# Norm factors by root and reciprocal, and small moves on GpSimd and VectorE, in a graph attention block that searches 64 MB of adjacency

## The chip, the cores and the metric

The kernel runs on one core of a Trainium2 chip. The metric is the device time of one execution in microseconds, taken as the median of three runs. Beside it stands one execution that the hardware profiler recorded; its span reaches from the first to the last instruction of the program.

## The reference, cut to what matters

```python
# x: 4096 x 512, adj: 4096 x 4096, W: 512 x (4 heads * 512), a: 4 x 1024 x 1
ht  = (h @ W).reshape(N, 4, 512).transpose(1, 0, 2)
src = einsum('hnd,hd->hn', ht, a[:, :512, 0]); dst = einsum('hnd,hd->hn', ht, a[:, 512:, 0])
e   = leaky_relu(src[:, :, None] + dst[:, None, :], 0.01) + adj[None]
h_prime = einsum('hij,hjd->hid', softmax(e, -1), ht).mean(0)
out = layernorm(x + h_prime)          # per row, eps 1e-5
```

The entries of adj reach 1e9, so in nearly every row the largest one outweighs everything else in the softmax, which is then one at a single column. The kernel computes that case: for every row i it finds the column c(i) of the largest entry of adj, fetches row c(i) of x, multiplies it by the mean of the four heads' weights, adds x and normalises. It also bounds how large the attention scores can be (from the norms of x, of W per head, and of a) and counts the rows whose lead over the second largest entry is too small for this. Only if there is one does it branch to `general`, which computes whole softmaxes. With these inputs the branch is not taken.

## The kernel before, in words

The 4096 rows are 32 blocks of 128 rows. Block 0 holds the rows 0 to 127; of the others, partition p holds 31 consecutive rows, one for each block. The scheduling is by hand: every engine runs its instructions in the order in which the program issues them, and the main loop is `for t in range(NB)` (line 523), a software pipeline of 32 steps. Step t does, in this order:

- SyncE (SP queue) issues the load of block t + 5 of adj (`load_adj`; 2 MB, in two pieces from block 28, in four for block 31) and, at some steps, four blocks of x (`load_x`) into `hold`, a tile that keeps all 32 blocks of x and later of the output. Six buffers hold adj.
- VectorE (DVE) reduces block t of adj to the maxima of segments of 16, 32 or 64 entries (`segment_maxima`, line 203: two instructions a block, four for block 31), finds the largest segment (`find_segment`, lines 210 and 212), and, in step t, looks for the column within the fetched segment of block t - 2 (`find_column`, line 263). In the steps of `END` the column comes after the segment, otherwise between the two reductions.
- GpSimd (POOL) works out the address of the leading segment and fetches it again from HBM with an indirect DMA (`fetch_segment`, lines 219 to 230), and, when the column is known, gathers the rows of x (`gather_rows`, lines 239 or 248). Two dependent indirect DMAs thus stand between the search of a block and its matmuls.
- TensorE (PE) turns the gathered rows of block t - 3 (`turn`, line 277; ScalarE copies the result to SBUF, line 279), adds x through the identity (`residual`, line 289) and multiplies by the mean weights (`products`, line 296: four matmuls of 128 x 512 in float32).
- ScalarE (ACT) takes the sums of squares for the bound (`row_norm`) and, in `parked_stats`, moves the result of block t - 4 into `hold` and takes its mean and variance.
- Every fourth step from step 8, `rstd` makes the factors 1/sqrt(var + eps) of four blocks with four POOL operations (lines 366 to 370, the power at line 367), and `finish` (line 375, ACT) normalises block t - 9.

Blocks 1 to 17 (`TABLED`) treat the first 128 rows of x apart, which are the columns found most often: the product of these 128 rows with the weights is kept in `z`, a one-hot matmul (`spread`, `from_table`) picks from it, and the gather skips these columns. To skip them, `gather_rows` adds 8192 to such a column (lines 245 and 247), so that it lies out of bounds and is not fetched.

The last blocks have their own order, written out after the loop (lines 586 to 652). Blocks 24 to 27 are put by (`put_by`) and get x by an addition on POOL or DVE (`add_x`, line 350), blocks 28 to 31 get their statistics on DVE (`moments`, `normalise`). The column of block 31 is searched in its whole row (line 271). The norms of heads for the bound (`head_norms`) are done in three parts in steps 24, 26 and 28, each behind the segment search. All stores stand behind the last loads on the SP queue; the last one is that of block 31.

Of the kernel before, what the change touches and what calls it, by code (L numbers as in the profile page):

```python
# [72 lines left out]
def leading_rows(ctx, tc, x, adj, W, a, out, ident, n_bad, any_bad):  # L73
# [44 lines left out]
    def pieces(ib):  # L118
        return PIECES if ib == NB - 1 else 2 if ib >= LATE else 1
# [55 lines left out]
    nc.gpsimd.iota(nth, pattern=[[0, 1]], base=0, channel_multiplier=-1)  # L175
# [20 lines left out]
    def segment_maxima(ib, lo, hi):  # L196

        e = spans[span_of(ib)][0]
        if lo == 0:
            seg_of[ib] = small.tile([P, N // e], F32, name=f"seg{e}", bufs=2)  # L200
        n = max(pieces(ib), 2)
        for k in range(lo * n // PIECES, hi * n // PIECES):
            nc.vector.tensor_reduce(  # L203
                seg_of[ib][:, ts(k, N // e // n)],
                adj_t[ib][:, ts(k, N // n)].rearrange("p (s e) -> p s e", e=e), axis=AX.X, op=OP.max,
            )
# [9 lines left out]
    def fetch_segment(ib):  # L216
        at = at_of.pop(ib)
        row = small.tile([P, 1], U32, name="row")
        nc.gpsimd.tensor_tensor(row, at[:, 0:1], first[:, ib : ib + 1], op=OP.add)  # L219
        k = span_of(ib)  # L220
        e = spans[k][0]
        lead = lead_pool.tile([P, e], F32, name=f"lead{e}", bufs=LEADS[k])
        nc.gpsimd.indirect_dma_start(  # L223
            out=lead, out_offset=None, in_=adj_segs[e],
            in_offset=bass.IndirectOffsetOnAxis(ap=row[:, :1], axis=0),
        )
        lead_of[ib] = lead
        if ib < NB - 1:
            start = at_of[ib] = small.tile([P, 1], U32, name="start")
            nc.gpsimd.tensor_tensor(start, at[:, 0:1], width[:, k : k + 1], op=OP.mult)  # L230
# [5 lines left out]
    def gather_rows(ib, col):  # L236
        if ib not in TABLED:
# [6 lines left out]
        away = small.tile([P, 1], U32, name="away")  # L244
        nc.gpsimd.tensor_scalar(away, col, float(P), float(SKIP), op0=OP.is_lt, op1=OP.mult)
        there = small.tile([P, 1], U32, name="there")
        nc.gpsimd.tensor_tensor(there, col, away, op=OP.add)  # L247
        nc.gpsimd.indirect_dma_start(  # L248
            out=y_t[ib], out_offset=None, in_=x,
            in_offset=bass.IndirectOffsetOnAxis(ap=there[:, :1], axis=0),  # L250
# [3 lines left out]
        nc.gpsimd.tensor_scalar(low, col, float(P), None, op0=OP.min)  # L254
# [109 lines left out]

    def rstd(i):
        nc.gpsimd.tensor_scalar(sd[:, i], sd[:, i], 1.0 / D, EPS, op0=OP.mult, op1=OP.add)
        nc.gpsimd.tensor_tensor(sd[:, i], sd[:, i], power[:, : i.stop - i.start], op=OP.pow)  # L367
        nc.gpsimd.tensor_mul(nm[:, i], nm[:, i], sd[:, i])
        if i.stop <= BEHIND:
            nc.gpsimd.tensor_scalar(sd[:, i], sd[:, i], -float(D), None, op0=OP.mult)  # L370

    def finish(ib):
        i = slice(ib, ib + 1)
        o = hold[:, ib, :] if ib < BEHIND else o_ps.pop(ib)
        nc.scalar.activation(hold[:, ib, :], o, AF.Identity, bias=nm[:, i], scale=sd[:, i])  # L375
# [144 lines left out]
    COLUMN, PROJECT, STATS, FINISH = 2, 3, 4, 8  # L520
    END = (*range(1, 3), *range(5, 20))

    for t in range(NB):
# [7 lines left out]
        middle = 1 if t == NB - 1 else 2  # L531
# [3 lines left out]
        segment_maxima(t, middle, PIECES)  # L535
# [8 lines left out]
        if t >= FINISH and t % Q == 0:  # L544
            rstd(slice(t - FINISH, t - FINISH + Q))
# [8 lines left out]
        if t in (24, 26, 28):  # L554
            head_norms((t - 24) // 2)
# [27 lines left out]
        if t > FINISH:  # L583
            finish(t - FINISH - 1)
# [36 lines left out]
    rstd(slice(BEHIND, BEHIND + 3))  # L621
# [34 lines left out]
def general(ctx, tc, x, adj, W, a, out, ident, n_bad):  # L656
# [21 lines left out]
    with ExitStack() as pre:  # L678
# [7 lines left out]
        for g in range(NCH):  # L686
            nc.gpsimd.dma_start(x_sb[:, ts(g, Q), :], x_blocks[:, ts(g, Q), :])
# [145 lines left out]
```

## Time and profile before

| | |
|---|---|
| median of three runs | 234.69 us (234.55 to 234.91) |
| the profiled execution's own time | 234.5 us |
| its span | 233.0 us |
| mean granted TensorE clock | 0.975 |
| busy: PE, DVE, ACT, POOL | 194.3, 191.1, 139.8, 112.9 us |
| moved by DMA | 96.45 MB, mean 414 GB/s |
| read from HBM, written to it | 88.54 MB, 8.39 MB |

A row of the profile names a line, an engine, an operation and its tiles as out<-in, then times in microseconds from the start of the span. Idle time before an instruction stands in brackets with what ended it. Rows of a group give the count, the busy time and the mean of one instruction in nanoseconds.

### The profile page before, as it was taken

The page shows a single profiled execution, that of the slowest core. Times are in us where ns is not written, and L with a number is a line of the kernel's source. Part 1 is how long each engine was busy: PE and PEld are TensorE (multiplying, and loading weights), DVE is VectorE, ACT ScalarE, POOL GpSimd, SP SyncE. Part 2 cuts the span into 40 slices and gives each one's busy share as a digit, 9 for nine tenths or more (in the row PEclk, how much of TensorE's full clock was granted, in tenths as well). Part 3 has the DMA queues.
Part 4 walks back from the last instruction along what each step waited for, and adds up shares of the span by engine and source line. Part 5 has one row for each costly group of instructions (what it writes and reads, how often), then busy time and mean ns, then how long its engine had stood idle before and what let it go on. Part 6 is the DMA issues. An engine that isn't in the chain of part 4 may idle for free.

```text
span 233.0 us, 2399 instructions
## 1 busy us (share of the span) xinstructions
PE 194.3 (83%) x570; PEld 92.6 (40%) x576; DVE 191.1 (82%) x301; ACT 139.8 (60%) x340; POOL 112.9 (48%) x260
## 2 busy tenths in 40 slices
PE   0069988789099996999899999999999977899990
PEld 0024443334044443445344444544443433345460
DVE  0448299899969997999799958977999999988782
ACT  3002213588077775699798767767756763289761
POOL 4020415615554875467657755653465447557210
PEclk9999999999769998899999999999999999999998
DMA  6999999999999999999999999999999999999985
GB/s 229 433 422 437 420 437 421 438 427 414 436 431 420 422 433 434 427 421 434 423 426 424 432 429 427 420 430 430 429 432 413 427 422 425 410 425 418 424 357 203
DMA packets 12834, 96.45 MB, mean 414 GB/s; under 512 B 2087, under 2 KB 2535, under 8 KB 7056
## 3 DMA queue, kind: packets, MB, share of 16 engines
q1 hardware_dynamic: 9216, 88.08, 89.5%
q0 software_dynamic: 3584, 8.16, 8.9%
q8 instruction: 5, 0.08, 0.1%
q14 instruction: 13, 0.11, 0.1%
q10 hardware_dynamic: 16, 0.02, 0.0%
HBM read 88.54 MB, written 8.39 MB: 416 GB/s over the span
## 4 chain that ended last, share of the span: by engine, by line
DMA 64%; DVE 19%; PE 6%; ACT 4%; issue 3%; POOL 1%; SPq 0%; DVEq 0%; POOLq 0%
DMA adj_t<-in_adj_dram 56%; DVE seg L203 16%; DMA hold<-in_L_gnn_W_dram 5%; PE o L296 4%; DMA y<-in_x_dram,col 3%; ACT sq L340 2%; PE o L384 2%; DVE at L212 1%; ACT hold L375 1%; DVE top L210 1%; PE tp L277 1%; DVE within L263 1%; POOL sd L367 0%; POOL lead L223 0%; ACT yt L279 0%
## 5 line engine op out<-in xcount | busy, mean ns | idle before, releaser
L203 DVE TENSOR_REDUCE seg<-adj_t 128x128 f32<-128x2048 f32 (+3 forms) x66 | 144.1, 2210 | 29.8 <-DMA adj_t<-in_adj_dram 29.7
L296 PE MATMUL o<-w_sum,yt 128*128 128x512 f32 x248 | 114.4, 602 | 2.0 <-ACT yt L279 1.8
L296 PEld LDWEIGHTS o<-w_sum,yt 128*128 128x128 f32 x248 | 46.3, 193 | 54.9 <-issue 42.6
L279 ACT COPY yt<-tp 128x512 f32<-128x512 f32 x33 | 19.1, 579 | 34.3 <-PE tp L277 34.3
L223 POOL DMA_INDIRECT lead<-in_adj_dram,row x32 | 32.6, 1020 | 13.1 <-POOL row L219 13.1
L277 PE MATMUL tp<-ident,y 128*128 128x128 f32 x128 | 22.5, 300 | 15.9 <-DMA y<-in_x_dram,there 12.0
L219 POOL TENSOR_TENSOR row<-at,first 128x1 uint32<-128x1 uint32 x32 | 6.1, 191 | 54.0 <-DVE at L212 45.4
L277 PEld LDWEIGHTS tp<-ident,y 128*128 128x128 f32 x128 | 18.7, 208 | 30.5 <-issue 27.0
L435 PE MATMUL o<-hold,ident 128*128 128x512 f32 x32 | 17.0, 699 | 13.7 <-DMA hold<-in_L_gnn_W_dram 13.7
L289 PE MATMUL o<-hold,ident 128*128 128x512 f32 x52 | 27.5, 614 | 0.0
L248 POOL DMA_INDIRECT y<-in_x_dram,there x17 | 18.9, 1111 | 10.9 <-POOL there L247 5.6
L340 ACT ACTIVATE sq<-hold 128x512 f32<-128x512 f32 x32 | 19.9, 624 | 0.0
L375 ACT ACTIVATE hold<-hold,nm,sd 128x512 f32<-128x512 f32 x24 | 19.1, 802 | 0.0
L239 POOL DMA_INDIRECT y<-in_x_dram,col x15 | 14.9, 995 | 7.6 <-POOL col L265 7.0
L363 ACT ACTIVATE sq<-hold,nm 128x512 f32<-128x512 f32 x24 | 17.4, 724 | 0.8
L435 PEld LDWEIGHTS o<-hold,ident 128*128 128x128 f32 x32 | 7.1, 226 | 22.8 <-issue 22.3
L436 ACT ACTIVATE w_sum<-o 128x512 f32<-128x512 f32 x4 | 2.4, 597 | 22.9 <-PE o L435 22.9
L326 ACT ACTIVATE off<-px,minus 128x128 f32<-128x128 f32 x17 | 6.3, 368 | 15.3 <-PE px L324 15.3
L361 ACT ACTIVATE hold<-o 128x512 f32<-128x512 f32 x24 | 14.3, 597 | 0.8
L336 PE MATMUL o<-z,pick 128*128 128x512 bf16 x46 | 13.9, 407 | 0.2
L210 DVE MAX8 top<-seg 128x8 f32<-128x256 f32 (+2 forms) x32 | 11.6, 361 | 1.1
L212 DVE FIND_INDEX8 at<-top,seg 128x8 uint32<-128x256 f32 (+2 forms) x32 | 11.3, 352 | 0.0
(113 smaller groups left out, 178.7 us busy)
## 6 DMA issues: line engine op xcount, KB each, us to landing
adj_t<-in_adj_dram SPq DMA_DIRECT2D x28, 2048.0 KB, 33.0
hold<-in_x_dram SPq DMA_DIRECT2D x6, 1024.0 KB, 32.4
adj_t<-in_adj_dram SPq DMA_DIRECT2D x6, 1024.0 KB, 28.1
hold<-in_L_gnn_W_dram SPq DMA_DIRECT2D x2, 2048.0 KB, 16.6
out_dram<-hold SPq DMA_DIRECT2D x7, 512.0 KB, 5.4
out_dram<-hold SPq DMA_DIRECT2D x3, 1024.0 KB, 15.1
adj_t<-in_adj_dram SPq DMA_DIRECT2D x4, 512.0 KB, 19.8
hold<-in_x_dram SPq DMA_DIRECT2D x2, 512.0 KB, 14.4
```

The source lines that it names most:

```text
L203: nc.vector.tensor_reduce(seg_of[ib][:, ts(k, N // e // n)], adj_t[ib][:, ts(k, N // n)].rearrange("p (s e) -> p s e", e=e), axis=AX.X, op ...
L223: nc.gpsimd.indirect_dma_start(out=lead, out_offset=None, in_=adj_segs[e], in_offset=bass.IndirectOffsetOnAxis(ap=row[:, :1], axis=0),)
L239: nc.gpsimd.indirect_dma_start(out=y, out_offset=None, in_=x, in_offset=bass.IndirectOffsetOnAxis(ap=col[:, :1], axis=0),)
L248: nc.gpsimd.indirect_dma_start(out=y_t[ib], out_offset=None, in_=x, in_offset=bass.IndirectOffsetOnAxis(ap=there[:, :1], axis=0), bounds_c ...
L277: nc.tensor.transpose(tp[:, kb, :], y[:, ds(kb, P, KB)], ident)
L279: nc.scalar.copy(yt, tp)
L289: nc.tensor.matmul(o_ps[ib], ident, hold[:, ib, :], start=start, stop=False)
L296: nc.tensor.matmul(o_ps[ib], yt_of[ib][:, kb, :], w_sum[:, kb, :], start=(start and kb == 0), stop=(kb == KB - 1),)
L340: nc.scalar.activation(sq, hold[:, ib, :], AF.Square, accum_out=xx[:, ib : ib + 1])
L363: nc.scalar.activation(sq, hold[:, ib, :], AF.Square, bias=nm[:, i], scale=-float(D), accum_out=sd[:, i])
L375: nc.scalar.activation(hold[:, ib, :], o, AF.Identity, bias=nm[:, i], scale=sd[:, i])
L435: nc.tensor.matmul(o, ident, hold[:, w_at + kb * H + h, :], start=(h == 0), stop=(h == H - 1))
```

## The change

1. **Factors.** `rstd` no longer takes a power on POOL. A new `root` issues a square root on ACT behind the statistics; three steps later `rstd` issues a reciprocal on DVE and two operations on POOL. The groups are blocks 0 to 3, 4 to 7, 8 to 11, 12 to 15, 16 to 19, and then 20 and 21, 22 and 23; their reciprocals stand in steps 10, 14, 18, 22, 26, 28 and 30. `finish` comes two steps later, with two blocks each in steps 28 and 29. Blocks 24 to 26 keep the power (`late_factors`).
2. **Skip with the segment.** For blocks 1 to 17 the 8192 is added to the segment's start in `fetch_segment` if the whole segment lies in the first 128 columns. The column then carries it, and the two operations in front of the gather go away. The one-hot pick is shifted by one to suit.
3. **Norms of heads** in steps 21, 22 and 23.
4. **Whole searches.** In steps 12 to 19 one reduction takes the whole block of adj.
5. In `general`, x is loaded in 16 pieces, not 8.

The diff, cut to its core:

```diff
-    nc.gpsimd.iota(nth, pattern=[[0, 1]], base=0, channel_multiplier=-1)
+    nc.gpsimd.iota(nth, pattern=[[0, 1]], base=-1, channel_multiplier=-1)
...
-        n = max(pieces(ib), 2)
+        n = max(pieces(ib), 1 if ib in WHOLE else 2)
...
-            nc.gpsimd.tensor_tensor(start, at[:, 0:1], width[:, k : k + 1], op=OP.mult)
+            if ib in TABLED:
+                away = small.tile([P, 1], F32, name="away")
+                nc.gpsimd.tensor_scalar(away, at[:, 0:1], float(P // e), float(SKIP), op0=OP.is_lt, op1=OP.mult)
+                nc.gpsimd.tensor_scalar(start, at[:, 0:1], float(e), away, op0=OP.mult, op1=OP.add)
+            else:
+                nc.gpsimd.tensor_tensor(start, at[:, 0:1], width[:, k : k + 1], op=OP.mult)
...
-        away = small.tile([P, 1], U32, name="away")
-        nc.gpsimd.tensor_scalar(away, col, float(P), float(SKIP), op0=OP.is_lt, op1=OP.mult)
-        there = small.tile([P, 1], U32, name="there")
-        nc.gpsimd.tensor_tensor(there, col, away, op=OP.add)
...
-        nc.gpsimd.tensor_scalar(low, col, float(P), None, op0=OP.min)
+        nc.gpsimd.tensor_scalar(low, col, float(SKIP - 1), float(SKIP - 1), op0=OP.max, op1=OP.subtract)
...
+    def root(i):
+        nc.scalar.activation(sd[:, i], sd[:, i], AF.Sqrt, bias=eps, scale=1.0 / D)
+
     def rstd(i):
+        nc.vector.reciprocal(sd[:, i], sd[:, i])
+        nc.gpsimd.tensor_mul(nm[:, i], nm[:, i], sd[:, i])
+        nc.gpsimd.tensor_scalar(sd[:, i], sd[:, i], -float(D), None, op0=OP.mult)
+
+    def late_factors(i):
         nc.gpsimd.tensor_scalar(sd[:, i], sd[:, i], 1.0 / D, EPS, op0=OP.mult, op1=OP.add)
         nc.gpsimd.tensor_tensor(sd[:, i], sd[:, i], power[:, : i.stop - i.start], op=OP.pow)
         nc.gpsimd.tensor_mul(nm[:, i], nm[:, i], sd[:, i])
-        if i.stop <= BEHIND:
-            nc.gpsimd.tensor_scalar(sd[:, i], sd[:, i], -float(D), None, op0=OP.mult)
...
-    COLUMN, PROJECT, STATS, FINISH = 2, 3, 4, 8
+    COLUMN, PROJECT, STATS, BEHIND_ROOT = 2, 3, 4, 3
+    FACTORS = (*((lo, lo + Q) for lo in range(0, BEHIND - Q, Q)), (BEHIND - 4, BEHIND - 2), (BEHIND - 2, BEHIND))
+    FINISHED = {t: (t - 11,) for t in range(11, 28)}
+    FINISHED |= {28: (17, 18), 29: (19, 20), 30: (21,), 31: (22,)}
+    WHOLE = range(12, 20)
...
-        middle = 1 if t == NB - 1 else 2
+        middle = PIECES if t in END else 1 if t == NB - 1 else 2
...
-        segment_maxima(t, middle, PIECES)
+        if t not in END:
+            segment_maxima(t, middle, PIECES)
...
-        if t >= FINISH and t % Q == 0:
-            rstd(slice(t - FINISH, t - FINISH + Q))
+        for lo, hi in FACTORS:
+            if t == hi - 1 + STATS + BEHIND_ROOT:
+                rstd(slice(lo, hi))
...
-        if t in (24, 26, 28):
-            head_norms((t - 24) // 2)
+        if 21 <= t < 24:
+            head_norms(t - 21)
...
-        if t > FINISH:
-            finish(t - FINISH - 1)
+        for lo, hi in FACTORS:
+            if t == hi - 1 + STATS:
+                root(slice(lo, hi))
+        for done in FINISHED.get(t, ()):
+            finish(done)
...
-    rstd(slice(BEHIND, BEHIND + 3))
+    late_factors(slice(BEHIND, BEHIND + 3))
...
-        for g in range(NCH):
-            nc.gpsimd.dma_start(x_sb[:, ts(g, Q), :], x_blocks[:, ts(g, Q), :])
+        for g in range(0, NB, 2):
+            nc.gpsimd.dma_start(x_sb[:, ds(g, 2), :], x_blocks[:, ds(g, 2), :])
```

More of the change, by code (lines that the diff above doesn't have):

```diff
@@ L243, in gather_rows @@
             return
-        away = small.tile([P, 1], U32, name="away")
-        nc.gpsimd.tensor_scalar(away, col, float(P), float(SKIP), op0=OP.is_lt, op1=OP.mult)
-        there = small.tile([P, 1], U32, name="there")
-        nc.gpsimd.tensor_tensor(there, col, away, op=OP.add)
         nc.gpsimd.indirect_dma_start(
             out=y_t[ib], out_offset=None, in_=x,
-            in_offset=bass.IndirectOffsetOnAxis(ap=there[:, :1], axis=0),
+            in_offset=bass.IndirectOffsetOnAxis(ap=col[:, :1], axis=0),
             bounds_check=N - 1, oob_is_err=False,
```

## The prediction

> **What bounds the kernel now.** I read the page first: its span and the row of DMA shares over 40 slices.
>
> ```profile
> span 233.0 us, 2399 instructions
> DMA  6999999999999999999999999999999999999985
> ```
>
> The sixteen DMA engines are at 90% or more in every slice except the first and the last two. Then the windows (columns after the window: its length, busy time and count of PE, weight loads, DVE, ACT and POOL, the granted clock, the DMA share, GB/s):
>
> ```profile
> 140.00:170.00 30.00, 29.71 (x91) 14.29 (x89) 26.01 (x42) 20.61 (x51) 14.33 (x29) 1.00 1.01 427
> 205.00:210.00 5.00, 4.74 (x14) 2.21 (x14) 4.62 (x10) 4.78 (x14) 2.46 (x4) 1.00 1.03 420
> 220.00:225.00 5.00, 5.00 (x19) 2.92 (x18) 4.46 (x10) 3.04 (x8) 1.28 (x3) 1.00 0.95 397
> 225.00:229.00 4.00, 2.27 (x11) 1.66 (x9) 2.92 (x12) 2.25 (x6) 0.00 (x0) 1.00 0.83 326
> 229.00:233.00 4.00, 0.00 (x0) 0.00 (x0) 0.15 (x1) 0.30 (x1) 0.00 (x0) 0.81 0.35 135
> ```
>
> The DMA share is full until about 220 us and falls only after that, to 0.83 and 0.35. The change moves no bytes. So time that an engine saves before the last rows of adj have landed is not time saved: DVE, idle for 4 of 30 us in the first window, would only wait longer for its rows. What counts is the order of events at the end, and there PE is the full engine (5.00 of 5.00). The chain that ended last says how PE's last work was released (start, us, what):
>
> ```profile
> 193.55 0.20 POOL start L230
> ...
> 193.84 0.20 POOL sd L366
> ...
> 194.11 1.06 POOL sd L367
> ...
> 195.24 0.20 POOL nm L368
> ...
> 195.52 0.23 POOL sd L370
> 195.76 0.17 POOL col L265
> ...
> 196.59 6.92 DMA y<-in_x_dram,col
> ...
> 203.64 0.72 PE tp L277 x4
> ...
> 223.73 3.55 PE o L384 x16
> ```
>
> This is step 28. POOL computes the factors of blocks 20 to 23 (L366 to L370) between the segment fetch of block 28 and the column of block 27. The gather of block 27 leaves behind them at 196.59, lands at 203.51, and PE turns block 27 at 203.64. From there PE runs almost without a gap to 227.28, the end of the last row. A gain at the end must pass here.
>
> **The change part by part.** *The factors of step 28.* Before, POOL is held from 193.84 to 195.76, 1.92 us, of which the power (L367) is 1.06. After, this step has two blocks and two POOL operations (L368 and L370, 0.20 and 0.23, with a gap of about 0.08 before each), behind a reciprocal on DVE. POOL, free at 193.75, is done with them at 194.26. The column then waits for DVE, whose search ends thus:
>
> ```profile
> 194.21 0.18 DVE L263 FIND_INDEX8 within<-top,lead 128x8 uint32<-128x32 f32 x1
> ...
> 200.44 0.96 POOL L239 DMA_INDIRECT y<-in_x_dram,col  x1 [0.54 <-POOL col L265]
> ```
>
> Search done at 194.39, column 0.07 later and 0.19 long, 0.54 from column to gather as in the second row: the gather of block 27 leaves at 195.2 rather than 196.59, and at 194.9 with the 0.3 us that DVE gains below. With its 6.92 us it lands at about 201.9. PE can take it no sooner than its residuals end:
>
> ```profile
> 200.67 1.88 PE L289 MATMUL o<-hold,ident 128*128 128x512 f32 x4
> ```
>
> They end at 202.55, so PE gains 1.09 us at block 27, and 1.3 if the gather of block 26, on which these residuals hang, lands earlier by DVE's 0.2 to 0.3.
>
> *DVE in the last steps.* A search (L212) and the adj reduction behind it, without and with the norms of heads between them:
>
> ```profile
> 180.62 0.28 DVE L212 FIND_INDEX8 at<-top,seg 128x8 uint32<-128x128 f32 x1
> ...
> 181.16 2.28 DVE L203 TENSOR_REDUCE seg<-adj_t 128x64 f32<-128x2048 f32 x1
> ...
> 186.30 0.28 DVE L212 FIND_INDEX8 at<-top,seg 128x8 uint32<-128x128 f32 x1
> 186.50 2.27 DVE L203 TENSOR_REDUCE seg<-adj_t 128x32 f32<-128x2048 f32 x1
> ...
> 191.56 0.22 DVE L212 FIND_INDEX8 at<-top,seg 128x8 uint32<-128x64 f32 x1
> ...
> 191.95 2.28 DVE L203 TENSOR_REDUCE seg<-adj_t 128x32 f32<-128x2048 f32 x1
> ```
>
> Step 27 has none: 0.20 from search to reduction, 0.14 for the shorter search of the last blocks (0.22 instead of 0.28). Step 26 has 0.54 and step 28 has 0.39: the parts moved away give back 0.34 and 0.25. The reciprocals come in at steps 26, 28 and 30:
>
> ```profile
> L404 DVE RECIPROCAL sd<-sd 128x1 f32<-128x1 f32 x5 | 0.8, 156 | 0.8 <-ACT sd L401 0.7
> ```
>
> I take 0.13 for each, since operations here start before the one ahead has quite ended; 0.16 at most for one column, and four columns should not be dearer by more than a few hundredths. So DVE is ahead by 0.2 after step 26, 0.3 after step 28, 0.2 after step 30. Each reciprocal waits for a root issued three steps earlier, which ACT finished about two steps before (a step is 5.4 us, from 186.50 to 191.95 above), so nothing is queued behind it. The three L203 rows bear no idle mark, so DVE does not wait for adj in these steps and the 0.3 us is real; it ends where the last quarter of block 31 lands.
>
> *The gate of block 29.* The new factors of step 30 (blocks 22, 23) stand before the column of block 29 on POOL:
>
> ```profile
> 204.24 0.20 POOL L230 TENSOR_TENSOR start<-at,width 128x1 uint32<-128x1 uint32 x1
> 204.67 0.19 POOL L265 TENSOR_TENSOR col<-start,within 128x1 uint32<-128x1 uint32 x1 [0.23 <-DVE within L263]
> 205.40 0.96 POOL L239 DMA_INDIRECT y<-in_x_dram,col  x1 [0.54 <-POOL col L265]
> 207.87 1.28 POOL L350 TENSOR_TENSOR adj_t<-adj_t,hold 128x512 f32<-128x512 f32 x1 [1.51 <-ACT sq L340]
> ...
> 214.31 0.96 POOL L239 DMA_INDIRECT y<-in_x_dram,col  x1 [0.61 <-PE tp L277]
> ```
>
> The start operation moves 0.3 earlier with DVE, to 203.94 to 204.14; two factor operations with their gaps (0.59) end at 204.73; column 0.19, then 0.54: gather at 205.46, against 205.40 before. Its landing time:
>
> ```profile
> DMA to landing us min/median/max: 7.0/7.0/7.0
> ```
>
> It lands at 212.5, and PE can turn block 29 then rather than at
>
> ```profile
> 213.07 0.63 PE L277 MATMUL tp<-ident,y 128*128 128x128 f32 x4
> ...
> 222.24 0.63 PE L277 MATMUL tp<-ident,y 128*128 128x128 f32 x4
> ```
>
> 213.07. Of the 1.1 to 1.3 us that PE gained, about 0.5 passes this gate. ACT, full in 205 to 210 (4.78 of 5), holds the same work as before in steps 30 and 31 and moves with PE; its two extra finishing operations fall in steps 28 and 29, where it waits for PE in any case:
>
> ```profile
> 197.35 0.59 ACT L279 COPY yt<-tp 128x512 f32<-128x512 f32 x1 [3.26 <-PE tp L277]
> ```
>
> *The gate of block 31.* Its gather (214.31, above) hangs on an addition of x on POOL (207.87), which comes after a load, and on DVE's search through a whole block. I take it as moved by 0.1 at most. It takes
>
> ```profile
> DMA to landing us min/median/max: 7.3/7.3/7.3
> ```
>
> so it lands at 221.6, and PE, which turns block 31 at 222.24 (above), can be 0.6 us early there and no more. From that turn to the end, 10.8 us, nothing is edited.
>
> *Edits that I cost at nothing.* The skip added with the segment takes one POOL operation out for blocks 1 to 17 and moves another ahead of the column; whole searches save one start of DVE in steps 12 to 19; the norms' new place puts three short parts on DVE in steps 21 to 23. All lie where DVE waits for landings:
>
> ```profile
> L203 DVE TENSOR_REDUCE seg<-adj_t 128x128 f32<-128x2048 f32 (+3 forms) x66 | 144.1, 2210 | 29.8 <-DMA adj_t<-in_adj_dram 29.7
> ```
>
> Were that cover gone they would be a gain of a few tenths each, the norms a loss of 0.6. The roots put seven short ACT operations in, each at most
>
> ```profile
> L401 ACT ACTIVATE sd<-mv,eps 128x1 f32<-128x1 f32 x5 | 1.4, 287 | 1.6 <-DVE mv L399 1.6
> L469 ACT ACT_TABLE_LOAD x1 | 1.3, 1283 | 0.0
> ```
>
> 0.29 us, and the table load of the root (1.28 us) moves from step 26 to step 7; ACT has over 9 us to spare in the 30 of 140 to 170. Finishing two steps later delays no store, because the stores queue behind the last loads. The loads in the general part do not run, since the test jumps over it.
>
> The Trainium skill, page "ScalarE: Activation LUTs", section "What ACT_TABLE_LOAD costs", gives about 2.66 us for a switch, the load of 1283 ns and a drain of about 1380 ns. This trace agrees on the load and, with 0.0 idle in the L469 row, shows no drain before it. With the skill's figure ACT would lose 2.7 us once in step 7, and the sum would be the same.
>
> **Sum.** Three gates in a row: 1.1 to 1.3 us at block 27, 0.5 at block 29, 0.6 at block 31. The smallest decides: 0.5 us, so a profiled span of 232.5 and a time of 234.0 in place of the profiled execution's 234.5 (1.5 us lie outside its span). The median before is 234.69, 0.19 above that execution; from it, 234.2. For this kernel 0.2%, 0.47 us, is about what a measurement can tell from no change (three runs lay 0.36 apart).
>
> **The rivals.** *Nothing comes through.* The landing times of all gathers of x lie far apart:
>
> ```profile
> DMA to landing us min/median/max: 6.1/8.2/9.2
> ```
>
> If that of block 29 or 31 takes 0.3 to 0.5 longer than before, its gate closes, and the time is 234.4 to 234.7. For it: the forecast rests on two landings. Against: it needs one that is slower still than the 7.0 or 7.3 of before, at the end, where both were under the median.
>
> *The gates stand open.* If block 29's gather lands in 6.1 us and block 31's is half a microsecond quicker too, PE keeps its 1.1 us: 233.6. Against it: both must be quicker at once.
>
> *Slower: the roots reload tables.* If the picks (line 328, the Relu of blocks 1 to 17) are not served by the root's table, each of the four roots before step 20 costs two loads, 2 times 1.28 us. No row shows a pick after the L469 load, so the trace cannot exclude it; squares and copies do run after it without a reload. ACT's idle time (9.4 of 30 us in the first window, 1.7 for a step of 5.4) would take up part of the 2.6, and PE, at 29.71 of 30 there, could not catch up the rest: 0.9 us at each root, 3.6 in all, of which its idle time ahead of block 27 (202.55 to 203.64) gives back 1.1, and with it goes the gain. That is 2.5 later: 237.2. It decides as soon as two such roots reload (1.8 against 1.1). The Trainium skill, page "ScalarE: Activation LUTs", section "Table sets: the hidden batching unit", says that cheap functions, relu and copy among them, are in every set. By that rule this rival falls; no run here shows it yet.
>
> *The change does not do what it says* can hardly be: the power leaves the loop in the diff itself. It can be true of the whole searches, which may leave the reduction's 2 times 2.2 us as it is; that is in the first rival.
>
> **How the numbers follow.** Forecast (0.3 to 0.7 us gained, 234.0 to 234.4) 0.58; nothing comes through 0.22; gates open 0.10; reload 0.04; 0.06 for a wait that I have not seen, to the slower side. The forecast's value sits just past 0.47 us, so 0.36 of its 0.58 counts as faster and 0.22 as same. Faster 0.36 + 0.10 = 0.46; same 0.22 + 0.20 = 0.42; slower 0.02 + 0.04 + 0.06 = 0.12. The range reaches from the open gates, 233.6, to short of the reload, 235.0.
>
> **What would show it.** Right: no power at step 28, block 27's gather near 195, its turn near 202.5; block 29's turn near 212.5 and waiting for its landing; one table load, at step 7; turn to end still 10.8 us. Wrong: a turn of block 31 no earlier than 222.2, loads beside later picks, or DVE waiting for PE at the norms of step 22.

## The result and the profile after

The changed kernel takes 237.11 us (median of 4 runs, 237.02 to 237.78), the kernel before 234.8 in the same comparison; the ratio is 1.01 with an interval of 1.008 to 1.0119. It is slower by 2.3 us, and 237.11 lies outside the predicted range of 233.6 to 235.0. The profiled execution took 237.78 us, and its page says:

```profile
span 233.6 us, 2385 instructions
DMA  6999999999999999999999999999999999999983
```

The first thing to see is what doesn't fit: the span is 0.6 us longer than before's 233.0, the time 3.3 us. Behind the span lie 237.78 - 233.6 = 4.18 us, where before has 1.5. The four runs have spans of 233.6, 233.1, 232.9 and 232.9 and 4.18, 4.05, 4.17 and 4.12 us outside them. So the loss is in a part of the time in which no instruction of the kernel runs.

Inside the span the events stand as the prediction has them. First POOL around the gathers of blocks 27, 29 and 31, then PE's turns of the same blocks, then ACT's last operation (start, us, what, idle before in brackets):

```profile
193.75 0.23 POOL L372 TENSOR_SCALAR sd<-sd 128x2 f32<-128x2 f32 x1
194.06 0.19 POOL L266 TENSOR_TENSOR col<-start,within 128x1 uint32<-128x1 uint32 x1
194.78 1.03 POOL L244 DMA_INDIRECT y<-in_x_dram,col  x1 [0.54 <-POOL col L266]
...
203.81 0.20 POOL L235 TENSOR_TENSOR start<-at,width 128x1 uint32<-128x1 uint32 x1
...
204.97 1.03 POOL L244 DMA_INDIRECT y<-in_x_dram,col  x1 [0.34 <-POOL col L266]
...
213.98 0.96 POOL L244 DMA_INDIRECT y<-in_x_dram,col  x1 [0.16 <-PE o L387]
```

```profile
202.35 0.63 PE L278 MATMUL tp<-ident,y 128*128 128x128 f32 x4
...
212.34 0.72 PE L278 MATMUL tp<-ident,y 128*128 128x128 f32 x4 [0.49 <-DMA y<-in_x_dram,col]
...
221.76 0.63 PE L278 MATMUL tp<-ident,y 128*128 128x128 f32 x4
```

```profile
228.26 0.56 ACT L431 ACTIVATE hold<-o,nm,sd 128x256 f32<-128x256 f32 x1 [0.43 <-DVE nm L413]
```

```profile
228.73 0.56 ACT L424 ACTIVATE hold<-o,nm,sd 128x256 f32<-128x256 f32 x1 [0.42 <-DVE nm L406]
```

The last row is that of before. The finish of block 31, behind which only its store is left, is 0.47 us earlier. From the end of that finish to the end of the span it is 233.0 - 229.29 = 3.71 us before and 233.6 - 228.82 = 4.78 after. So for the two profiled executions the sum is -0.47 up to the last finish, +1.07 for the store behind it, and +2.68 outside the span: +3.28.

What goes on outside the span can be asked of the DMA view, from 233.6 to 240 us of the kernel after (40 slices of 0.16 us, then the queues):

```profile
DMA  0000000000000000041000000000000000000000
...
DMA packets 3, 0.02 MB, mean 4 GB/s; under 512 B 0, under 2 KB 0, under 8 KB 0
...
q14 instruction: 3, 0.02, 1.6%
```

and of before, from 233 to 240:

```profile
DMA packets 0, 0.00 MB, mean 0 GB/s; under 512 B 0, under 2 KB 0, under 8 KB 0
```

After the last instruction, in slices 18 and 19 (about 236.4 us, 2.8 us behind the end of the span), the chip fetches three pieces of instructions, none under 8 KB. Before fetches none there. Inside the span after fetches no more than before: two pieces come between 230 and 232 us in both, and in all there are 11 pieces on this queue in after and 13 in before.

### The profile page after: what moved, and what is told of

The parts are those of the page before. It is cut to its first block, busy times and chain, and to the rows that moved or that the text cites. A ratio compares the mean times of both kernels' runs of the same rounds, so it can differ in the third digit from the quotient of the medians.

```text
span 233.6 us, 2385 instructions
## 1 busy us (share of the span) xinstructions
PE 192.6 (82%) x570; PEld 91.3 (39%) x576; DVE 191.2 (82%) x300; ACT 142.0 (61%) x347; POOL 103.5 (44%) x233
## 4 chain that ended last, share of the span: by engine, by line
DMA 66%; DVE 24%; PE 3%; issue 3%; POOL 1%; ACT 0%; SPq 0%; DVEq 0%
DMA adj_t<-in_adj_dram 56%; DVE seg L203 18%; DMA hold<-in_L_gnn_W_dram 5%; DMA lead<-in_adj_dram,row 5%; PE o L297 2%; PE o L391 2%; DVE at L212 1%; DVE col L272 1%; DVE top L210 1%; DVE within L264 1%; POOL lead L223 0%; DVE inner L258 0%; ACT hold L431 0%; PE tp L278 0%; DVE halves_st L425 0%
## 5 line engine op out<-in xcount | busy, mean ns | idle before, releaser
L203 DVE TENSOR_REDUCE seg<-adj_t 128x128 f32<-128x2048 f32 (+5 forms) x58 | 143.7, 2496 | 30.0 <-DMA adj_t<-in_adj_dram 29.8
L297 PEld LDWEIGHTS o<-w_sum,yt 128*128 128x128 f32 x248 | 45.8, 191 | 54.1 <-issue 42.0
L442 PE MATMUL o<-hold,ident 128*128 128x512 f32 x32 | 16.1, 660 | 14.3 <-DMA hold<-in_L_gnn_W_dram 14.3
L290 PE MATMUL o<-hold,ident 128*128 128x512 f32 x52 | 27.3, 611 | 0.0
L249 POOL DMA_INDIRECT y<-in_x_dram,col x17 | 18.3, 1076 | 5.5 <-POOL col L266 4.9
L244 POOL DMA_INDIRECT y<-in_x_dram,col x15 | 14.9, 994 | 7.0 <-POOL col L266 6.8
L442 PEld LDWEIGHTS o<-hold,ident 128*128 128x128 f32 x32 | 6.6, 213 | 22.9 <-issue 21.3
L337 PE MATMUL o<-z,pick 128*128 128x512 bf16 x46 | 13.2, 391 | 0.5 <-ACT pick L329 0.2
```

The source lines that it names most:

```text
L203: nc.vector.tensor_reduce(seg_of[ib][:, ts(k, N // e // n)], adj_t[ib][:, ts(k, N // n)].rearrange("p (s e) -> p s e", e=e), axis=AX.X, op ...
L244: nc.gpsimd.indirect_dma_start(out=y, out_offset=None, in_=x, in_offset=bass.IndirectOffsetOnAxis(ap=col[:, :1], axis=0),)
L249: nc.gpsimd.indirect_dma_start(out=y_t[ib], out_offset=None, in_=x, in_offset=bass.IndirectOffsetOnAxis(ap=col[:, :1], axis=0), bounds_che ...
L290: nc.tensor.matmul(o_ps[ib], ident, hold[:, ib, :], start=start, stop=False)
L297: nc.tensor.matmul(o_ps[ib], yt_of[ib][:, kb, :], w_sum[:, kb, :], start=(start and kb == 0), stop=(kb == KB - 1),)
L442: nc.tensor.matmul(o, ident, hold[:, w_at + kb * H + h, :], start=(h == 0), stop=(h == H - 1))
```

## The experiments

**The theories.** Theory A: the change moves the place at which GpSimd's program ends, counting the instructions of `general`, which the branch jumps over; at the new place the last instructions have to be fetched after the end of the work, and that costs 2.6 us. Rival B: 16 loads in `general` cost something as such. Rival C: the length of another engine's program, or of all together, decides. Rival D: the edited operations that run cause it. For the time inside the span the theory is that the 0.47 us is real and the store's way through full DMA engines takes it back; its rival is that the gain was the scatter of one execution.

One thing has to be known for reading the numbers: some executions of a kernel take about 1 us more than its others (19 of the 114 of before that were measured beside the experiments, at 235.4 us or more), so a median of ten moves by some tenths. In four profiles of versions of after the clock granted to PE falls to half for about 3.4 us, which is one cause (last section); no profile shows a long execution of before. The part outside the span doesn't scatter like this, and is the better measure where the place of the code is asked for.

**Loads of the general part, both ways** (`before_general16`, and `after_general8`, which is the same edit backwards on the kernel after):

```diff
-        for g in range(NCH):
-            nc.gpsimd.dma_start(x_sb[:, ts(g, Q), :], x_blocks[:, ts(g, Q), :])
+        for g in range(0, NB, 2):
+            nc.gpsimd.dma_start(x_sb[:, ds(g, 2), :], x_blocks[:, ds(g, 2), :])
```

> The kernel before with only the change in the part that never runs (x loaded in 16 pieces instead of 8). What it executes is the same as before. Place-of-code theory (the 2.6 us that the changed kernel spends after its span are fetches of instructions, and depend on how many instructions stand in each engine's program, executed or not): 234.7 or up to 2.7 us more, whichever side of a fetch block the end falls on; outside the span 1.5 or about 4.2 us. Theory that the 16 loads themselves cost it (more queues or descriptors set up): 237.3, outside 4.2. Theory that an executed edit costs it (table of the root, power gone): 234.7, outside 1.5.

> The changed kernel with that part as before (8 pieces). Place of code: what is executed is the same, so the span stays at 233.0 to 233.6; outside it 1.5 or 4.2. Theory of the 16 loads: outside 1.5, time 234.5. Theory of an executed edit: 237.1, outside 4.2.

Before with 16 pieces: 234.51 us, ratio 1.0007 (0.9989 to 1.0026), 234.36 for a span of 232.7 in the profile. After with 8 pieces: 234.45, ratio 0.9983 (0.9963 to 1.0003), 234.43 for a span of 232.9. The slowdown is gone in the second and doesn't come in the first: sixteen loads as such cost nothing, against rival B, and all the edits that run are still in the second, against rival D.

**Only the length of a program** (`after_pool6`; `after_dve16` is the same with 16 of `nc.vector.memset`). The instructions stand in `general` and never run:

```diff
         a_rows = alone.tile([2 * H, D], F32, name="a_rows_g")
+        spare = alone.tile([P, 1], F32, name="spare")
+        for _ in range(6):
+            nc.gpsimd.memset(spare, 0.0)
```

> The changed kernel with six memsets on GpSimd added to the part that never runs, which bring GpSimd's program back to the length that it has in the kernel before. Place of code with GpSimd as the engine: outside the span falls from 4.2 to 1.5, time 234.3. If another engine's end is the one that is misplaced: 237.1 as the changed kernel. Theories of the 16 loads or of an executed edit: 237.1, outside 4.2.

> The changed kernel with sixteen memsets on VectorE added to the part that never runs. Place of code with GpSimd as the engine: no change, 237.1, outside 4.2. With VectorE as the engine: outside moves, to 1.5 or further up. Theories of the 16 loads or of an executed edit: 237.1, outside 4.2.

Six memsets that never run, on GpSimd, take the slowdown away: 234.35 us, ratio 0.9989 (0.9973 to 1.0006). The DMA view of `after_pool6` from 233 to 240:

```profile
DMA packets 0, 0.00 MB, mean 0 GB/s; under 512 B 0, under 2 KB 0, under 8 KB 0
```

Sixteen on DVE don't: 238.0, ratio 1.014 (1.0117 to 1.0164), 238.12 for a span of 234.0, with three fetches behind it as in the kernel after. The median is 0.9 above the 237.1 that was expected: the spans are longer (233.6 to 234.0 in the four runs). The profiled one has a fall of the clock (last section); for the others no trace shows why. Outside the span lie 4.11 to 4.31 us in all four. That is against rival C for DVE's program; it is GpSimd's that counts.

**A second place** (`after_general12`: four loads fewer than after).

```diff
-        for g in range(0, NB, 2):
-            nc.gpsimd.dma_start(x_sb[:, ds(g, 2), :], x_blocks[:, ds(g, 2), :])
+        lo = 0
+        for n in (3, 3, 3, 3, 3, 3, 3, 3, 2, 2, 2, 2):
+            nc.gpsimd.dma_start(x_sb[:, ds(lo, n), :], x_blocks[:, ds(lo, n), :])
+            lo += n
```

> The changed kernel with x loaded in 12 pieces in the part that never runs, between the 8 that gave 234.45 and the 16 that gave 237.11. Place of code: one or the other, 234.4 or 237.1, nothing between; it tells on which side of this length the edge lies. Theory that the number of loads costs by itself: 235.8, half way.

234.61 us, ratio 1.0003 (0.9988 to 1.0018), 235.83 for a span of 234.2: nothing behind the span. So four loads fewer do as well as eight loads fewer or six memsets more; the harmful stretch is narrow.

**The same place in the kernel before** (`before_pool523`). GpSimd's program of before is cut down to as many instructions as that of after, again only in `general`:

```diff
-        for g in range(NCH):
-            nc.gpsimd.dma_start(x_sb[:, ts(g, Q), :], x_blocks[:, ts(g, Q), :])
-        for kb in range(KB):
-            nc.gpsimd.dma_start(w_sb[:, kb, :], w_blocks[:, kb, :])
+        for g in range(4):
+            nc.gpsimd.dma_start(x_sb[:, ts(g, NB // 4), :], x_blocks[:, ts(g, NB // 4), :])
+        nc.gpsimd.dma_start(w_sb, w_blocks)
...
-        nc.gpsimd.dma_start(r, x_of)
+        nc.scalar.dma_start(r, x_of)
```

> The kernel before, with fewer instructions on GpSimd in the part that never runs (x and W there in fewer pieces, one load moved to ScalarE's queue), so that GpSimd's whole program is exactly as long as in the changed kernel, 13 instructions shorter than before. All that runs is the kernel before. If the absolute length of GpSimd's program decides (its end spills over the edge of a block of instructions that has not been fetched): 237.1, 4.2 us outside the span, three fetches after its end. If it also takes the changed kernel's shorter main part (the jump over the part that never runs starts 21 instructions later here), or an edit that runs: 234.5, 1.6 outside.

236.9 us, ratio 1.0103 (1.0088 to 1.0117), 236.86 for a span of 232.7: 4.16 outside. Its DMA view from 233 to 240:

```profile
DMA  0000000000000001200000000000000000000000
...
DMA packets 3, 0.02 MB, mean 4 GB/s; under 512 B 0, under 2 KB 0, under 8 KB 0
```

The instructions that run are those of before, and the whole slowdown is there, with the three fetches. This settles the cause: not one of the edits that run, but how long GpSimd's program is, and so where it ends. (The load that moves to ScalarE's queue lengthens ScalarE's program here; `after_general8` and `after_general12` change GpSimd's loads alone.)

**The same place, one block on** (`before_pool115` has 108 memsets of the kind above in the kernel before, `after_pool128` 121 in the kernel after). If the pattern repeated every 128 instructions, both would stand at the harmful place again.

> The kernel before with memsets on GpSimd in the part that never runs, so many that GpSimd's program is 115 instructions longer. With the 13 that it is longer than in the changed kernel, that makes 128: if instructions are fetched in blocks of 128 (8 KB packets of 64 bytes each), its end falls at the same place of a block as in the changed kernel. Place of code: 237.1, 4.2 us outside the span, three fetches after the span's end, though everything that runs is the kernel before. Theory that an edit that runs costs the 2.6 us: 234.5, outside 1.6.

> The changed kernel with memsets on GpSimd in the part that never runs that make its program 128 instructions longer: the end stands at the same place of a block of 128 as in the changed kernel, one block further from the jump. If the place within a block alone decides: 237.1, 4.2 outside. If a jump into a block that is not there yet fetches that block and the next, as the run with 115 more on the kernel before suggests (234.91, 1.9 outside): 234.4 to 234.8, 1.6 to 1.9 outside, with a fetch near 225 in the trace.

It doesn't repeat: 234.91 us, ratio 1.0015 (1.0005 to 1.0026), and 234.8, ratio 1.0014 (1.0001 to 1.0027). Neither has a packet behind the span. In both, 1.9 us lie outside the span in the profile (235.11 for 233.2, 235.13 for 233.2), 0.3 to 0.4 more than in the harmless versions. A piece fetched at 225 to 227 us, which was expected for `after_pool128`, is there in both, but in before and `after_pool6` too, so it decides nothing. The strict form of theory A was wrong here. All lengths side by side, with every run:

| version | GpSimd's program, in instructions more than in after | outside the span, us |
|---|---|---|
| after_general8 | -8 | 1.52 to 1.70 |
| after_general12 | -4 | 1.52 to 1.63 |
| after | 0 | 4.05 to 4.18 |
| after_dve16 | 0 | 4.11 to 4.31 |
| before_pool523 | 0 | 4.02 to 4.16 |
| before | 13 | 1.50 to 1.70 |
| after_pool6 | 13 | 1.51 to 1.67 |
| before_general16 | 21 | 1.53 to 1.66 |
| before_pool115 | 128 | 1.89 to 2.03 |
| after_pool128 | 128 | 1.86 to 2.04 |

The three versions of one length are slow, whichever kernel they come from, and no other is. Which places cost 2.6, 0.3 or nothing beyond these stays open.

**What the edits that run are worth** (`after_pow`: the power back in `rstd`, roots and reciprocals out; `after_norms`: norms of heads back in steps 24, 26 and 28, on `after_pool6`). Neither has fetches behind its span.

```diff
     def rstd(i):
-        nc.vector.reciprocal(sd[:, i], sd[:, i])
-        nc.gpsimd.tensor_mul(nm[:, i], nm[:, i], sd[:, i])
+        late_factors(i)
         nc.gpsimd.tensor_scalar(sd[:, i], sd[:, i], -float(D), None, op0=OP.mult)
...
-        for lo, hi in FACTORS:
-            if t == hi - 1 + STATS:
-                root(slice(lo, hi))
```

```diff
-        if 21 <= t < 24:
-            head_norms(t - 21)
+        if t in (24, 26, 28):
+            head_norms((t - 24) // 2)
```

> The changed kernel with the power on GpSimd back in the factors (no root, no reciprocal; groups and steps as changed, two blocks in steps 28 and 30), its code in a harmless place. My theory of the gain (GpSimd's queue at steps 28 and 30 gates the gathers of blocks 27 and 29): gather of block 27 at about 196.0 instead of 194.8, gather of block 29 a microsecond later than 205.0, and the issue of the last store back at 229.3 or later, 0.5 us behind the changed kernel's 228.8. Rival (the gain comes from DVE, by the norms' move): last store still at 228.8 to 228.9.

> The changed kernel, its code in a harmless place, with the norms of heads back in steps 24, 26 and 28. My theory: DVE is 0.6 us later in the last steps (0.34 and 0.25), the column and gather of block 29 move by 0.3 to 0.5, and the last store is issued at 229.1 to 229.3. Rival (GpSimd's factors alone make the gain): 228.8.

`after_pow` takes 234.91 us, ratio 1.0012 (1.0 to 1.0024). Its POOL around the gather of block 29, and PE's turns of blocks 29 and 31:

```profile
204.72 0.72 POOL L375 TENSOR_TENSOR sd<-sd,power 128x2 f32<-128x2 f32 x1
205.53 0.20 POOL L376 TENSOR_TENSOR nm<-nm,sd 128x2 f32<-128x2 f32 x1
...
206.56 1.09 POOL L244 DMA_INDIRECT y<-in_x_dram,col  x1 [0.36 <-POOL col L266]
```

```profile
213.94 0.72 PE L278 MATMUL tp<-ident,y 128*128 128x128 f32 x4 [1.34 <-DMA y<-in_x_dram,col]
...
222.96 0.63 PE L278 MATMUL tp<-ident,y 128*128 128x128 f32 x4
```

With the power in steps 28 and 30 the gather of block 27 leaves at 195.87 us, about as expected, and that of block 29 1.59 us later than in the kernel after (206.56 against 204.97), PE waits 1.34 us for it, and block 31 is turned 1.2 us later (222.96 against 221.76). The gate of block 29 is as the working has it. The later groups alone, with the power, are no better than before and perhaps slightly worse; it is the cheap factors that make them harmless.

`after_norms` takes 234.46 us, ratio 1.0007 (0.9993 to 1.002); without the edit (`after_pool6`) it was 0.9989 (0.9973 to 1.0006). The intervals overlap. Its gather of block 27 leaves at 195.10 us, that of `after_pool6` at 194.66; first `after_norms`, then `after_pool6`:

```profile
195.10 1.02 POOL L244 DMA_INDIRECT y<-in_x_dram,col  x1 [0.54 <-POOL col L266]
```

```profile
194.66 1.02 POOL L244 DMA_INDIRECT y<-in_x_dram,col  x1 [0.54 <-POOL col L266]
```

That is 0.44 us (0.32 against after's 194.78), about the 0.3 of DVE's time in the prediction. The gather of block 29 moves likewise, from 204.85 to 205.29, as expected. The last finish is at 229.27, where the store's issue was expected, but this can't be put down to the norms, since PE's clock fell in that execution (last section).

**Where the 0.47 goes** (`before_less`, `after_less`: without the store of blocks 16 to 19, whose rows of the output stay unwritten; `before_less4`, `after_less4`: without the stores of blocks 8 to 23, unwritten likewise). Those of after stand on `after_pool6`.

```diff
-    for ib in range(4 * Q, BEHIND, Q):
+    for ib in range(5 * Q, BEHIND, Q):
         store(nc.sync, ib, Q)
```

```diff
-    for ib in range(2 * Q, 4 * Q, 2):
-        store(nc.sync, ib, 2)
-    for ib in range(4 * Q, BEHIND, Q):
-        store(nc.sync, ib, Q)
```

> The kernel before without the store of blocks 16 to 19 (1 MB of the output stays unwritten). It is the base for the next run. If the stores queued ahead hold up the last one, its landing comes sooner after its issue than the 2.45 us of before and the time falls by some tenths of a microsecond; if not, 234.5.

> The changed kernel with the six idle memsets that mend the place of its code, and without the store of blocks 16 to 19. Theory that the 0.5 us gained up to the issue of the last store are given back to stores that are still under way: with 1 MB less under way the gain comes through, 0.4 to 0.5 us below the kernel before with the same store left out. Rival, that the last store's landing is slow for another reason (its own 256 KB, the write's receipt): the two stay 0.1 apart.

> The kernel before without the stores of blocks 8 to 23 (4 MB of the output stay unwritten), the base of the next run. Stores under way as the cause: the last store lands about 2 us after its issue at 229.3, not 2.45, and the span falls by 0.3 to 0.5; DMA is far from full after 215 us. Its own landing as the cause: 2.4 to 2.5 as before.

> The changed kernel with its code in a harmless place (six idle memsets), without the stores of blocks 8 to 23. Stores under way as the cause: the last store lands as soon after its issue as in the kernel before with the same stores left out, and the two differ by the whole 0.5 us (0.2%). Its own landing as the cause: it lands 0.4 or more later after its issue than there, and the two differ by 0.1 to 0.2.

234.89 us for `before_less` (ratio 1.0011, 0.9991 to 1.0031; four of its twelve runs take 235.3 us or more, and its fastest was 233.93), 233.84 for `after_less` (0.9962, 0.9943 to 0.9981), 233.97 for `before_less4` (0.9984, 0.9963 to 1.0005), 233.35 for `after_less4` (0.9947, 0.9935 to 0.9959). The windows at the end (PE, weight loads, DVE, ACT, POOL, clock, DMA share, GB/s), first of after, then of `after_less4`:

```profile
220.00:225.00 5.00, 5.00 (x20) 3.16 (x19) 4.40 (x11) 2.86 (x6) 1.14 (x3) 1.00 0.94 392
225.00:229.00 4.00, 1.79 (x9) 1.23 (x7) 2.65 (x9) 2.07 (x5) 0.00 (x0) 0.98 0.91 366
229.00:233.00 4.00, 0.00 (x0) 0.00 (x0) 0.00 (x0) 0.00 (x0) 0.00 (x0) 0.50 0.24 92
```

```profile
220.00:225.00 5.00, 5.00 (x21) 3.32 (x20) 4.43 (x12) 3.27 (x7) 1.15 (x3) 1.00 0.31 120
225.00:229.00 4.00, 1.39 (x7) 0.88 (x5) 2.26 (x8) 1.67 (x4) 0.00 (x0) 1.00 0.78 311
```

The other stores are still under way when the last one is issued: the DMA share from 225 to 229 is 0.91 (0.83 before), with the same bytes to move. Without the stores of blocks 8 to 23 it is 0.31 from 220 to 225. The table sets ACT's last finish (rows as above; end is start plus 0.56) beside the span:

| kernel | last finish ends | span | from one to the other |
|---|---|---|---|
| before | 229.29 | 233.0 | 3.71 |
| before_general16 | 228.87 | 232.7 | 3.83 |
| before_pool115 | 229.20 | 233.2 | 4.00 |
| before_pool523 | 229.16 | 232.7 | 3.54 |
| after | 228.82 | 233.6 | 4.78 |
| after_pool6 | 228.72 | 232.8 | 4.08 |
| after_general8 | 228.40 | 232.9 | 4.50 |
| after_pool128 | 228.88 | 233.2 | 4.32 |
| before_less | 229.39 | 233.0 | 3.61 |
| after_less | 228.87 | 232.4 | 3.53 |
| before_less4 | 228.71 | 232.1 | 3.39 |
| after_less4 | 228.42 | 231.8 | 3.38 |

All of these have the full clock from 190 to 204 us. With all stores, the last finish is at 229.13 in the mean of four versions that run the code of before and at 228.71 for after, 0.42 earlier (within each four they lie up to 0.5 apart), but the spans are 232.9 and 233.1 in the mean: the way behind it is longer by 0.65. Four more profiles of versions of after, with all stores, have a later last finish and less behind it: `after_norms` 229.27 and 3.53, `after_pow` 230.02 and 3.58, `after_dve16` 230.48 and 3.52, `after_general12` 230.67 and 3.53. In all these profiles with all stores the stretch is at least 3.5 us and the span at least 232.7, so an earlier finish mostly lengthens the stretch behind it.

Without the store of blocks 16 to 19, and without those of blocks 8 to 23, the last stretch is the same for both kernels (3.61 and 3.53; 3.39 and 3.38) and the gain reaches the end: 0.6 and 0.3 us of span. In the medians the pairs are 234.89 - 233.84 = 1.05 and 233.97 - 233.35 = 0.62 apart, more than the 0.4 to 0.5 expected; but the two versions of before have long executions (four and two of twelve take 235.3 us or more) and those of after have none. The fastest executions are 0.27 and 0.35 apart. One expectation failed: with one store less the median of before doesn't fall. So a gain of about 0.4 us at the last finish is there in the mean, and the drain of the stores takes most of it back. That is shown for means and pairs of versions, not for a single execution: why the profiled execution of after needed 4.78 where `after_pool6` needed 4.08 is scatter that no run explains.

**Another queue for the last store** (`before_actstore`, and `after_actstore` on `after_pool6`):

```diff
-    store(nc.sync, NB - 1, 1)
+    store(nc.scalar, NB - 1, 1)
```

> The kernel before with the store of block 31 issued from ScalarE's queue instead of SyncE's. If the last store waits in SyncE's queue behind the stores of blocks 26, 27 and 30: it lands sooner, 234.0 to 234.3. If the DMA engines are just full, whoever issues: 234.5.

> The changed kernel, code in a harmless place, with the store of block 31 on ScalarE's queue. If the last store waits in SyncE's queue: it lands by 230.8 to 231.0 instead of 231.6, and the gain of 0.5 comes through: 233.7 to 233.9, 0.3% below the kernel before. If the DMA engines are just full: 234.3.

234.71 us, ratio 1.0011 (0.9995 to 1.0028), and 235.09, ratio 1.0013 (0.9992 to 1.0034; fastest 234.1). There is no gain in either, so it isn't the place in SP's queue that holds the last store. The second is 0.8 above the 234.3 that full DMA engines would give. Its profiled execution has a fall of PE's clock; why most of its runs are so long is open.

The best versions found are `after_general8` and `after_pool6`, the change without its slowdown. Against before they are at 0.9983 and 0.9989 with intervals up to 1.0003 and 1.0006: 0.3 to 0.4 us less in the ratio, not told apart from no change.

## Why the prediction was wrong

The step that failed is in the sum: "1.5 us lie outside its span". It was carried over from before to after as if it were a constant; it became 4.1 to 4.2. The sentence that should have raised the question is "The loads in the general part do not run, since the test jumps over it", costed at nothing. That they don't run is right. But they are part of GpSimd's program, and so are the operations that the change takes out; together they bring its end to a place where 2.6 us go by before the time stops. None of the rivals had this mechanism; 0.06 had been left for "a wait that I have not seen, to the slower side", and the rival with a similar time, 237.2 by table reloads, is not what happened.

*Block 27*: predicted gather at 194.9 to 195.2 and turn near 202.5; measured 194.78 and 202.35. Right.

*Block 29*: predicted gather at 205.46, landing at 212.5, with PE waiting; measured gather at 204.97, turn at 212.34 after 0.49 us of waiting for the landing. The gate is right. The gather left 0.49 us sooner than predicted (the operation for the segment's start begins at 203.81 and not 203.94, and from the column to the gather POOL idles 0.34 and not 0.54), but from gather to turn it is 7.37 us, not 7.0.

*Block 31*: predicted landing at 221.6, the gather moved by 0.1 at most, and the turn 0.5 to 0.6 earlier than 222.24; measured gather 0.33 earlier (213.98 against 214.31), turn at 221.76, 0.48 earlier, without waiting for a landing. The size is right by luck, for another wait sets it. PE's rows from the turn of block 30 on, first of before, then of after:

```profile
217.81 0.75 PE L277 MATMUL tp<-ident,y 128*128 128x128 f32 x4
...
219.41 0.22 PE L508 MATMUL px<-gap,ones 128*1 128x32 f32 x2
```

```profile
216.93 0.75 PE L278 MATMUL tp<-ident,y 128*128 128x128 f32 x4
...
218.93 0.22 PE L515 MATMUL px<-gap,ones 128*1 128x32 f32 x2 [0.40 <-DVE gap L511]
```

At the turn of block 30 PE is 0.88 ahead. Then it waits 0.40 us for `gap`, the test of the rows' leads that DVE works out and PE counts. The prediction has no gate there. DVE, ahead by over a microsecond at 203 us, had itself waited 0.65 us for the last quarter of block 31 (from 205.67 to 206.32), which is where the prediction lets its gain end. `after_pool6` has this wait too (0.28 us), `after_general8` and `after_pool128` don't.

*The way behind it.* "Turn to end still 10.8 us" fails: 233.6 - 221.76 = 11.84. Up to the last finish it held (6.49 from the turn to the finish's start before, 6.50 after); the store behind it did not. "From that turn to the end, 10.8 us, nothing is edited" is true of the instructions and passes over what they share. The other stores are in the DMA engines when the last one is issued, and the prediction's own window from 225 to 229, with a DMA share of 0.83, already showed it. It took the engines as full until about 220 us and the stretch behind that as free.

*Reload rival*: it falls. The groups of after:

```profile
L367 ACT ACTIVATE sd<-sd,eps 128x4 f32<-128x4 f32 (+1 forms) x7 | 2.1, 297 | 0.2
...
L367 ACT ACT_TABLE_LOAD x1 | 1.3, 1283 | 0.0
...
L370 DVE RECIPROCAL sd<-sd 128x4 f32<-128x4 f32 (+1 forms) x7 | 1.1, 156 | 0.0
```

One load at the first of seven roots, 1283 ns, none at the picks behind it; roots and reciprocals cost 297 and 156 ns, as taken (0.29, and 0.13 to 0.16). By the rule of the Trainium skill, page "ScalarE: Activation LUTs", section "Table sets: the hidden batching unit", relu is in every set; this trace agrees.

Two slips in the sums change nothing: with 0.59 us for two factor operations and their gaps POOL would be done at 194.34 in step 28 and not at 194.26, and a landing at 212.46 leaves 0.6 us at block 29, not 0.5.

Without the failed step the forecast would still have been a little too good. Against the base of its own comparison, 234.46, a gain of 0.47 to 0.5 makes 234.0; the harmless versions of the change take 234.35 and 234.45. The mechanism inside the kernel was right up to block 29, a gain of the forecast size was found at the last finish, for a reason that was in part another, and 0 to 0.4 of it reaches the time.

## What to carry to other kernels

Compare the time with the span before explaining anything by an engine: if the part outside the span has moved, look for fetches behind the last instruction in the DMA view, and test with a few instructions that never run on one engine's program. Code that is jumped over is not always free: at one length it cost 2.6 us here, at the others next to nothing. And where the last transfer stands behind others in full DMA engines, what an engine saves ahead of it counts only as far as those have drained.

## What the runs showed of the hardware

**Fetches behind the end.** Where GpSimd's program ends, with code that never runs counted in, can cost 2.6 us: three pieces of instructions fetched about 3 us after the last instruction, in `after`, `after_dve16` and `before_pool523`; in the runs of all other versions no more than 2.04 us lie outside the span. Four loads fewer or six memsets more avoid it. The Trainium skill, page "Runtime: NRT & Kernel Launch", section "Instruction fetch mechanics", says that instructions are fetched in sequence, in blocks, and that a branch taken to a place outside the blocks at hand has to wait for a fetch. The runs agree in kind, for the branch over `general` is such a jump to the end of the program; that the jump is what waits is argued, not shown, since no row names the instruction that waits behind the span, nor the engine whose instructions these pieces hold.

**The clock after a pause of PE.** PE's row of block 25 in `after_norms`, and its windows (length, PE busy, granted clock, DMA share, GB/s):

```profile
192.31 0.83 PE L278 MATMUL tp<-ident,y 128*128 128x128 f32 x4 [2.35 <-DMA y<-in_x_dram,col]
```

```profile
190.00:192.00 2.00, 0.00 (x0) 1.00 0.98 407
192.00:194.00 2.00, 1.69 (x6) 0.69 0.99 414
194.00:196.00 2.00, 2.00 (x3) 0.50 1.04 434
196.00:198.00 2.00, 2.00 (x6) 0.96 1.03 430
```

and the same of after:

```profile
192.34 0.72 PE L278 MATMUL tp<-ident,y 128*128 128x128 f32 x4 [2.41 <-DMA y<-in_x_dram,col]
```

```profile
192.00:194.00 2.00, 1.66 (x7) 1.00 1.00 418
194.00:196.00 2.00, 2.00 (x6) 1.00 1.03 430
```

A pause of 2.35 us, while a gather of x lands late, is followed by half the clock for about 3.4 us (the lack of 0.31, 0.50 and 0.04 over 2 us each makes 1.7 us of full clock); a pause of 2.41 in after is not. Pauses of 2.13 us in `after_dve16`, 2.33 in `after_actstore` and 2.46 in `after_general12` were followed by it, one of 2.74 in `after_pow` was not. In the four executions with the fall the last finish is later than the 228.40 to 228.88 of the four versions of after in the table: 229.27 and 229.45 where the pause is before block 25 (`after_norms`, `after_actstore`), 230.48 and 230.67 where it is before block 26 (`after_dve16`, `after_general12`). So a gather a little later than usual can cost PE between a few tenths and 2 us, or nothing. It is one cause of the scatter; whether the long executions of before have the same one is not shown. The Trainium skill, page "TensorE: Matmul & The Clock Gate", section "What's actually happening", has a free-running window of about 3.4 us, and says that PE goes to half the clock after at least one idle window. The length agrees, and a free phase would explain why like pauses end differently; but here 2.1 to 2.5 us of pause were enough, less than a whole window.
